# Two-layer attention and expert kernel: expert result rows scattered by token and loaded plainly, instead of gathered by the output stage

## The chip, the cores and the metric

The kernel runs on one core of a Trainium2 chip. A core has five engines with a queue each: TensorE (PE, with its weight loads as PEld), VectorE (DVE), ScalarE (ACT), GpSimd (POOL) and SyncE (SP), and 16 DMA engines that move data on behalf of the queues. The metric is the time of one execution in device microseconds (us): the median of 14 runs is 753.95 us (748.63 to 759.43).

## The reference

Input x has 8 sequences of 512 tokens with 128 channels, all in float32. Two layers follow each other, each `x = x + attention(norm(x)) + experts(norm(x))`.

- Layer 0: a linear attention with a feature map and two states that are multiplied, and a top-1 choice among 8 experts (one 128 x 128 product each, weighted by the router's probability).
- Layer 1: a windowed attention (16 heads, window 32) with a remote part over 64 pooled latents, and a top-2 choice among 8 experts with a hidden layer of 512:

```python
logits = x_flat @ gate_w.T
probs = softmax(logits)
topk_probs, topk_idx = top_k(probs, 2)
hidden = relu(einsum('th,ehf->tef', x_flat, w1) + b1)
all_out = einsum('tef,efh->teh', hidden, w2) + b2
y = sum(gathered(all_out, topk_idx) * topk_probs[:, :, None], axis=1)
```

The change touches the layer-1 experts alone.

## The kernel before, in words

**Stages.** `layer0(b)` (line 626) and `attention1(b)` (line 761) work on one sequence b. The layer-1 experts work on groups of four sequences (GB = 4, line 33), so there are two groups h. `route(h)` (line 968) sorts the 4096 token-and-choice pairs of a group by expert, on the chip: every expert gets a whole number of tiles of 128 rows, 39 tiles in all (TILES, line 35), and the rows of a tile that no token fills are padding. It makes `place_i` (line 1062), which says for every token and choice in which row of the sorted order it lies, and `token_i` (lines 1101 to 1106), which says for every sorted row which token it comes from. `token_i` comes out of a one-hot product `inv` (lines 1073 to 1099): for each sorted row the token's number in its block of 128 ("within") and the number of the block ("tile").

`experts1(h)` (line 1112) goes over the 39 tiles. For each four tiles it gathers the input rows by token from `x_rows` in DRAM (four indirect DMAs on POOL, tile `xgt`, lines 1153 to 1163) and transposes them on PE (`tpx`). For each tile SP loads the weights of its expert (`w1` and `w2` of 256 KB, `b2` of 64 KB, lines 1118 to 1151, with three to four buffers each); PE makes the hidden layer `hp` (line 1192), ACT the relu `ht`, PE the product `yp` (line 1207), and DVE adds the bias to it in `ys` (line 1216). Four tiles of `ys` go in one plain store to `y_rows` in DRAM, in sorted order, on SP (lines 1217 to 1222).

`output(b)` (line 1225) is the last stage of a sequence. It gathers, for each of the two choices a and each of the four blocks t of 128 tokens, the rows of `y_rows` that belong to these tokens: eight indirect DMAs on POOL into `yg` (lines 1232 to 1238), 64 in the whole kernel. DVE then adds each block, times its weight `gw`, to x1 (eight instructions a sequence, line 1243), and SP stores x1 to the output (line 1246). As `y_rows` is one tensor of a group, the first gather of a group waits until all its tiles are stored.

**What sets the order.** Every instruction is recorded first (class `Recorder`, line 113; each call goes through line 348, so that almost all instructions have this line in the profile). `Recorder.order` (line 221) then makes the order in which the instructions of all sequences and stages are put into the engines' queues. It takes, at each step, the instruction that can start first by a table of costs (`_duration`, line 354), and among these the one with the lowest rank; an instruction's rank comes from the time window of its stage in a table written by hand (`PLAN`, line 1256). On the chip each queue is worked off strictly in that order. Nothing is waited for except data and buffers.

**Names in the profile.** `xgt` input rows of a tile, `hp`, `ht`, `yp`, `ys` as above; `sc`, `m`, `pt`, `pw`, `pv` the steps of the windowed attention (scores, softmax, transposed weights, masked weights, product); `le`, `rem_p` those of its remote part; `loc`, `aT`, `fp` its last steps; `amx`, `asd`, `ard`, `lrd` the maxima, sums and divisors of the softmaxes; `xg`, `rp`, `gbc` the experts of layer 0.

Of the kernel before, what the change touches and what calls it, by code (L numbers as in the profile page):

```python
# [9 lines left out]
F32 = mybir.dt.float32  # L10
# [8 lines left out]
P = 128  # L19
# [3 lines left out]
E = 8  # L23
# [6 lines left out]
CHUNK = N // NLAT  # L30


GB = 4
GT = GB * NT
TILES = (2 * GB * N + E * (P - 1)) // P
NEG = -1.0e30
SCALE = 1.0 / float(np.sqrt(np.float32(D)))
SCALE_LAT = 1.0 / float(np.sqrt(np.float32(LC // LH)))
# [3 lines left out]
def _columns(widths):  # L42
    at, out = 0, {}
    for name, w in widths:
# [18 lines left out]
        ("before", P), ("iota", P), ("part4", 1), ("chunk4", NFC), ("within", 1), ("tile", GT),  # L63
    ]
)

# [1 line left out]
def _constants():  # L68

    c = np.zeros((P, _CN), np.float32)  # L70
    p = np.arange(P)

    def put(name, a):
        lo, hi = _CCOL[name]
        c[: a.shape[0], lo:hi] = a.reshape(a.shape[0], hi - lo)

    put("ident", np.eye(P))
    put("heads", p[:, None] // D == p[None, :] // D)
    put("head4", (p[:, None] // D) % 4 == np.arange(4)[None, :])
# [12 lines left out]
    put("late", late)  # L92
    put("group", group)
    put("first", np.broadcast_to(E - np.arange(E), (P, NT, E)))
    put("before", p[:, None] < p[None, :])
    put("iota", np.broadcast_to(p, (P, P)))
    put("part4", p[:, None] // NFC)
    put("chunk4", p[:, None] % NFC == np.arange(NFC)[None, :])
    put("within", p)
    put("tile", np.broadcast_to(np.arange(GT), (P, GT)))  # L100
    return c


# [285 lines left out]
def two_layers_kernel(  # L389
# [55 lines left out]
    def ct(name):  # L445
        lo, hi = _CCOL[name]
        return csb[:, lo:hi]
# [170 lines left out]


    middle, late = {}, {}  # L620
    x_rows = [dram.tile([GB * N, C], F32, tag="xr", name=f"x_rows_{h}", bufs=2) for h in range(B // GB)]
    y_rows = [dram.tile([TILES * P, C], F32, tag="yr", name=f"y_rows_{h}", bufs=2) for h in range(B // GB)]
    logits = [keep.tile([P, GT, E], F32, tag="logits", name=f"logits_{h}") for h in range(B // GB)]
    places = {}

    def layer0(b):
# [114 lines left out]

        xn2 = work.tile([P, NT, C], F32, tag="oT", name="xn2" + nm, bufs=1)
        layernorm(xn2, x1, "d" + nm)
        h, hb = divmod(b, GB)
# [223 lines left out]
    def route(h):  # L968


        nm = f"_{h}"
        n2 = 2 * GT
        sh = [P, 2, GT, E]
        pick = small.tile(sh, F32, tag="picked", name="picked" + nm, bufs=1)
# [20 lines left out]
        mm(tot[:, : GT * E], ones, mf)  # L995
        yield

        half = GT // 2
# [63 lines left out]
        place_i = small.tile([P, n2], I32, tag="place_i", name="place_i" + nm)  # L1062
# [12 lines left out]
        for q in range(n2 // step):  # L1075
            ts = slice(q * step, (q + 1) * step)
            ohr = work.tile([P, step, P], BF16, tag="xg0", name=f"ohr{nm}_{q}", bufs=1)
            nc.vector.tensor_tensor(
                ohr, ct("iota").unsqueeze(1).to_broadcast([P, step, P]),
                rf[:, ts].unsqueeze(2).to_broadcast([P, step, P]), ALU.is_equal,  # L1080
            )
            shj = [P, step, TILES]
            ohj = small.tile(shj, BF16, tag="ohj", name=f"ohj{nm}_{q}", bufs=1)
            nc.vector.tensor_tensor(
                ohj, ct("iota")[:, :TILES].unsqueeze(1).to_broadcast(shj),
                jf[:, ts].unsqueeze(2).to_broadcast(shj), ALU.is_equal,
            )
            tw = small.tile([P, 2, step, TILES], BF16, tag="tw", name=f"tw{nm}_{q}", bufs=1)
            t0 = (q * step) % GT
            nc.vector.tensor_scalar_mul(tw[:, 0], ohj, ct("within"))  # L1090
            nc.gpsimd.tensor_tensor(
                tw[:, 1], ohj, ct("tile")[:, t0 : t0 + step].unsqueeze(2).to_broadcast(shj), ALU.mult
            )
# [13 lines left out]
        places[h] = (place_i, token_i, gw, bias, own_i)  # L1107
        yield

    QUAD, AHEAD = 4, 3  # L1110

    def experts1(h):

        nm = f"_{h}"
        _, token_i, _, bias, own_i = places[h]
        ws, xgs, xts, hts, numbers = {}, {}, {}, {}, {}

        def fetch(j):
# [34 lines left out]
        def gather(q):  # L1153
# [8 lines left out]
                )  # L1162
            xgs[q] = xg

        def turn(q):
# [18 lines left out]
        for j in range(TILES + 1):  # L1184
# [20 lines left out]
            if j:  # L1205
                ht, (_, w2k, b2) = hts.pop(j - 1), ws.pop(j - 1)
                yp = bank(f"yp{nm}_{j - 1}")
                for k in range(NFC):
                    mm(
                        yp[:, :C], ht[:, k], w2k[:, k],  # L1210
                        start=k == 0, stop=k == NFC - 1,
                    )
                q, a = divmod(j - 1, QUAD)
                if a == 0:
                    ys = work.tile([P, QUAD, C], F32, tag="ys", name=f"ys{nm}_{q}", bufs=2)
                nc.vector.tensor_add(ys[:, a], yp[:, :C], b2)
                if a == QUAD - 1 or j == TILES:
                    r0 = q * QUAD * P
                    nc.sync.dma_start(
                        y_rows[h][r0 : r0 + (a + 1) * P].rearrange("(t p) c -> p t c", p=P),  # L1220
                        ys[:, : a + 1],
                    )
                yield

    def output(b):

        nm = f"_{b}"
        x1 = late.pop(b)
        h, hb = divmod(b, GB)
        place_i, _, gw, _, _ = places[h]  # L1230
# [18 lines left out]
    def load_next(b):  # L1249
# [16 lines left out]
        "attention1": (  # L1266
            (105, 168), (147, 199), (206, 258), (273, 318),
            (319, 432), (431, 481), (481, 538), (554, 633),
        ),
        "experts1": ((262, 436), (426, 546)),  # L1270
        "output": (
            (413, 488), (441, 502), (481, 482), (436, 471),
            (489, 595), (570, 580), (547, 625), (578, 664),
        ),
    }

    def put(name, stage, arg, at):
        nc.begin(*PLAN[name][at])
        for _ in stage(arg):
            pass  # L1280
# [3 lines left out]
            put("load", load_next, b, b - 1)  # L1284
        put("layer0", layer0, b, b)
    for name, stage, n in (
        ("route", route, B // GB), ("attention1", attention1, B),
        ("experts1", experts1, B // GB), ("output", output, B),
    ):
        for i in range(n):  # L1290
            put(name, stage, i, i)
# [62 lines left out]
```

## Time and profile before

| what | value |
|---|---|
| median of 14 runs | 753.95 us (748.63 to 759.43) |
| the profiled execution: time / span from first to last instruction | 756.32 us / 754.2 us |
| mean granted PE clock | 0.857 of full |
| busy time in the span: PE, PEld | 587.8 us (78%), 435.9 us (58%) |
| DVE, ACT, POOL | 512.7 us (68%), 339.4 us (45%), 379.2 us (50%) |
| moved by DMA | 86.65 MB, mean 115 GB/s |
| the 78 gathers of input rows on POOL: busy, mean of one | 78.5 us, 1006 ns |
| the 64 gathers of result rows on POOL: busy, mean of one | 62.0 us, 969 ns |
| the 64 updates of x1 by `yg` on DVE: busy, mean of one | 30.9 us, 499 ns |

The profile shows one execution. Busy time counts instructions at work; a queue that waits is idle. A row of the timelines gives start and length in us, engine, line, operation, `out<-in` by the program's names, and in brackets the idle time before it and what ended it ("issue" is time in which the engine waited for nothing that the profile shows). The chain of work that ended last goes back from the last instruction, at each step to what released it. Busy shares are means over stages that have different limits, so the tables by stretch matter more than the sums. The time of an indirect DMA on POOL is the making of its descriptors; the landing of the data comes later.

### The profile page before, as it was taken

To read this page: it belongs to the slowest core of one execution; us is meant where nothing else is said; L and a number is where in the kernel's file an instruction comes from. 1 tells how busy PE (TensorE), PEld (TensorE's weight loads), DVE (VectorE), ACT (ScalarE), POOL (GpSimd) and SP (SyncE) were. 2 spreads that over 40 slices of the span, in tenths; PEclk is the share of its full clock that TensorE was granted. 3 is DMA by queue.
4 is the path that set the end of the run, shared out by engine and by line. 5 is a ranking of instruction groups with operands and counts; after the bars stand their busy time and mean duration, and the time that the engine had idled before them with its cause. 6 is when DMAs were issued, how large, how long until landed. Compare 5 with 4: busy or idle time off the path is not lost.

```text
span 754.2 us, 14113 instructions
## 1 busy us (share of the span) xinstructions
PE 587.8 (78%) x4869; PEld 435.9 (58%) x4869; DVE 512.7 (68%) x1258; ACT 339.4 (45%) x877; POOL 379.2 (50%) x376
## 2 busy tenths in 40 slices
PE   4387798868968769889989989887798789797512
PEld 2233454536736435775756768766687668784412
DVE  2736779899699896984888774993529644616662
ACT  2225246344652332582563767443555447353500
POOL 1021132645551357835755345267668875606784
PEclk9687696998896768898999999999969988997555
DMA  4110212112011221445546465966758775771011
GB/s 139 70 42 29 77 51 89 40 54 75 15 43 57 76 78 55 114 129 133 151 114 185 132 194 158 249 165 191 210 149 218 204 206 146 184 199 50 26 47 51
DMA packets 101543, 86.65 MB, mean 115 GB/s; under 512 B 8056, under 2 KB 80576, under 8 KB 101472
## 3 DMA queue, kind: packets, MB, share of 16 engines
q1 hardware_dynamic: 96640, 75.43, 34.3%
q0 software_dynamic: 4544, 9.32, 5.2%
q10 hardware_dynamic: 288, 1.00, 0.4%
q8 instruction: 39, 0.64, 0.3%
q14 instruction: 32, 0.26, 0.1%
HBM read 76.28 MB, written 9.44 MB: 114 GB/s over the span
## 4 chain that ended last, share of the span: by engine, by line
PE 34%; DVE 28%; POOL 13%; ACT 11%; DMA 7%; issue 6%; POOLq 0%; DVEq 0%; ACTq 0%
PE rp L348 5%; PE yp L348 4%; PE hp L348 4%; POOL yg L348 3%; PE hk L348 2%; DVE nt L348 2%; PE rem_p L348 2%; POOL pw L348 2%; DVE k L348 2%; ACT vb L348 2%; POOL xgt L348 2%; DVE x L348 2%; ACT ks L348 2%; DVE nr L348 2%; DVE ks L348 2%
## 5 line engine op out<-in xcount | busy, mean ns | idle before, releaser
L348 ACT ACTIVATE ht<-hp,bias 128x128 f32<-128x128 f32 x312 | 90.9, 370 | 53.9 <-PE hp L348 53.5
L348 POOL DMA_INDIRECT xgt<-x_rows,token_i x78 | 78.5, 1006 | 33.1 <-issue 15.3
L348 POOL TENSOR_TENSOR xg<-xT,gbc 128x512 f32<-128x512 f32 x32 | 44.0, 1375 | 100.7 <-DMA gbc<-gd 65.4
L348 PE MATMUL hp<-xt,w 128*128 128x128 f32 x624 | 88.0, 286 | 7.5 <-DVE m L348 2.3
L348 PEld LDWEIGHTS hp<-xt,w 128*128 128x128 f32 x624 | 79.3, 198 | 19.2 <-issue 6.3
L348 PE MATMUL yp<-w,ht 128*128 128x128 f32 x624 | 86.6, 287 | 0.6 <-ACT ht L348 0.5
L348 POOL DMA_INDIRECT yg<-y_rows,place_i x64 | 62.0, 969 | 45.2 <-DMA y_rows<-ys 19.4
L348 PEld LDWEIGHTS yp<-w,ht 128*128 128x128 f32 x624 | 79.4, 200 | 3.9 <-issue 1.9
L348 PE MATMUL rp<-xg,we_sb 128*128 128x512 f32 x128 | 73.8, 676 | 3.8 <-DVE x2p L348 1.9
L348 PE MATMUL pv<-pw,vb 128*32 128x64 f32 (+1 forms) x1088 | 40.0, 235 | 42.3 <-POOL pw L348 42.0
L348 PEld LDWEIGHTS pv<-pw,vb 128*32 128x32 f32 x1088 | 36.2, 123 | 50.1 <-POOL pw L348 47.2
L348 POOL TENSOR_TENSOR pw<-pt,csb 128x512 f32<-128x512 f32 x32 | 49.0, 1531 | 13.2 <-DVE pt L348 10.7
L348 DVE SCALAR_TENSOR_TENSOR x<-yg,gw,x 128x128 f32<-128x128 f32 x64 | 30.9, 499 | 29.0 <-DMA yg<-y_rows,place_i 28.4
L348 POOL TENSOR_TENSOR m<-m,ard 128x512 f32<-128x512 f32 x32 | 35.4, 1111 | 27.6 <-DVE ard L348 12.4
L348 POOL TENSOR_TENSOR m<-m,amx 128x512 f32<-128x512 f32 x32 | 35.4, 1106 | 27.0 <-DVE amx L348 24.3
L348 POOL TENSOR_TENSOR le<-le,lrd 128x128 f32<-128x128 f32 (+3 forms) x32 | 23.8, 749 | 34.3 <-DVE lrd L348 18.1
L348 ACT ACTIVATE m<-m,zero_b 128x512 f32<-128x512 f32 x32 | 23.1, 724 | 38.2 <-POOL m L348 38.1
L348 DVE TENSOR_TENSOR ys<-yp,b 128x128 f32<-128x128 f32 x78 | 20.9, 275 | 28.3 <-PE yp L348 22.6
L348 DVE TENSOR_TENSOR xg<-xT,gbc 128x512 f32<-128x512 f32 x32 | 25.8, 805 | 20.8 <-PE rp L348 18.7
L348 ACT ACTIVATE le<-le,zero_b 128x128 f32<-128x128 f32 (+3 forms) x32 | 18.0, 562 | 48.2 <-DVE le L348 45.2
L348 ACT COPY vb<-v 32x128 f32<-32x128 f32 x128 | 37.7, 295 | 2.8 <-PE pv L348 1.0
L348 PE MATMUL hk<-xn,ks 128*128 128x129 f32 x128 | 24.1, 364 | 18.7 <-DVE ks L348 18.7
(218 smaller groups left out, 1314.3 us busy)
## 6 DMA issues: line engine op xcount, KB each, us to landing
w<-in_w_dram SPq DMA_DIRECT2D x156, 256.0 KB
gbc<-gd SPq DMA_DIRECT2D x64, 256.0 KB
b<-in_experts_b_dram SPq DMA_DIRECT2D x78, 64.0 KB
y_rows<-ys SPq DMA_DIRECT2D x18, 256.0 KB
x<-in_x_dram SPq DMA_DIRECT2D x8, 256.0 KB
x_rows<-xn SPq DMA_DIRECT2D x8, 256.0 KB
out_dram<-x SPq DMA_DIRECT2D x8, 256.0 KB
xgt<-x_rows,token_i POOLq DMA_INDIRECT x78
```

Of the source, the lines that this page charges most:

```text
L348: r.ENGINES[name], lambda: call(*args, **kwargs), aps[:1], aps[1:], time, delay, shape
```

## The change

- `route` numbers the token blocks of both choices through: the constant "tile" now holds 1 to 32 (choice 0: 1 to 16, choice 1: 17 to 32), where it held 0 to 15 for both. From the same one-hot product it so gets `row_i`, the row of every sorted row in a tensor with two planes (one for each choice) of 2048 rows behind 128 spare rows; padding gives row 0. `token_i` is made from it: minus 2048 for the second plane, minus 128, not under 0. These are six small DVE instructions in place of two. `place_i` is no longer used outside `route`.
- `experts1` has a `ys` for each tile (six buffers) and sends it by an indirect DMA on POOL to the rows `row_i` of `y_rows`: 39 scatters a group in place of 10 plain stores on SP. `y_rows` is a DRAM tensor that the recorder doesn't follow. After the last tile DVE writes one column of each of the last six `ys` and copies it to `done`: that write can't be made before the scatter that reads the `ys` has landed.
- `output` copies `done` into `yg`, so that the loads that overwrite `yg` come after it, and loads the rows of the sequence in two plain transfers of 256 KB on SP, in place of eight gathers on POOL.
- Groups are written as a table (still four and four), and all windows of `PLAN` but "load" have new numbers, so the order of all queues is a new one.

```diff
-GB = 4
-GT = GB * NT
-TILES = (2 * GB * N + E * (P - 1)) // P
+GROUPS = (4, 4)
...
-    put("tile", np.broadcast_to(np.arange(GT), (P, GT)))
+    n = 2 * max(GROUPS) * NT
+    put("tile", np.broadcast_to(1 + np.arange(n), (P, n)))
...
+        y_rows.append(tc.nc.dram_tensor(f"y_rows_{h}", [P + 2 * n * N, C], F32, kind="Internal").ap())
...
-        own_p = small.tile([P, TILES], F32, tag="own_p", name="own_p" + nm, bufs=1)
-        nc.vector.tensor_copy(own_p, inv[:, :TILES])
-        nc.vector.scalar_tensor_tensor(
-            token_i, inv[:, TILES : 2 * TILES], float(P), own_p, ALU.mult, ALU.add
-        )
-        places[h] = (place_i, token_i, gw, bias, own_i)
+        nc.vector.tensor_copy(at_tile, inv[:, : 2 * TILES].rearrange("p (a j) -> p a j", j=TILES))
+        nc.vector.tensor_single_scalar(other, at_tile[:, 1], float(GT) + 0.5, ALU.is_gt)
+        nc.vector.scalar_tensor_tensor(row, at_tile[:, 1], float(P), at_tile[:, 0], ALU.mult, ALU.add)
+        nc.vector.scalar_tensor_tensor(other, other, -float(GT * P), row, ALU.mult, ALU.add)
+        nc.vector.tensor_scalar(token_i, other, -float(P), 0.0, ALU.add, ALU.max)
+        nc.vector.tensor_copy(row_i, row)
+        places[h] = (row_i, token_i, gw, bias, own_i)
...
+        def scatter(j, ys):
+            ids = row_i[:, j : j + 1]
+            def store():
+                tc.nc.gpsimd.indirect_dma_start(
+                    y_rows[h], bass.IndirectOffsetOnAxis(ap=ids, axis=0), ys, None
+                )
+            nc.add("POOL", store, [], [ys, ids], 1.25, 2.4)
+            last[:] = (last + [ys])[-YS:]
...
-                if a == 0:
-                    ys = work.tile([P, QUAD, C], F32, tag="ys", name=f"ys{nm}_{q}", bufs=2)
-                nc.vector.tensor_add(ys[:, a], yp[:, :C], b2)
-                if a == QUAD - 1 or j == TILES:
-                    r0 = q * QUAD * P
-                    nc.sync.dma_start(
-                        y_rows[h][r0 : r0 + (a + 1) * P].rearrange("(t p) c -> p t c", p=P),
-                        ys[:, : a + 1],
-                    )
+                ys = work.tile([P, C], F32, tag="ys", name=f"ys{nm}_{j - 1}", bufs=YS)
+                nc.vector.tensor_add(ys, yp[:, :C], b2)
+                scatter(j - 1, ys)
                 yield
+        for i, ys in enumerate(last):
+            nc.vector.memset(ys[:, :1], 0.0)
+            nc.vector.tensor_copy(done[:, i : i + 1], ys[:, :1])
+        written[h] = done
+        yield
...
         yg = work.tile([P, 2, NT, C], F32, tag="yg", name="yg" + nm, bufs=1)
+        nc.vector.tensor_copy(yg[:, 0, 0, :YS], written[h])
+        rows = y_rows[h][P:].rearrange("(a t p) c -> p a t c", a=2, p=P)
         for a in range(2):
-            for t in range(NT):
-                col = a * GT + hb * NT + t
-                nc.gpsimd.indirect_dma_start(
-                    yg[:, a, t], None, y_rows[h],
-                    bass.IndirectOffsetOnAxis(ap=place_i[:, col : col + 1], axis=0),
-                )
+            nc.sync.dma_start(yg[:, a], rows[:, a, hb * NT : (hb + 1) * NT])
...
         "layer0": (
-            (41, 43), (57, 70), (60, 174), (113, 194),
-            (180, 254), (261, 270), (310, 335), (331, 344),
+            (51, 52), (82, 83), (80, 130), (83, 164),
+            (147, 220), (253, 290), (276, 338), (361, 362),
         ),
-        "route": ((230, 231), (348, 407)),
+        "route": ((211, 216), (399, 444)),
...
-        "experts1": ((262, 436), (426, 546)),
+        "experts1": ((238, 447), (481, 579)),
         "output": (
-            (413, 488), (441, 502), (481, 482), (436, 471),
-            (489, 595), (570, 580), (547, 625), (578, 664),
+            (465, 533), (442, 443), (474, 493), (524, 525),
+            (639, 692), (562, 577), (584, 585), (661, 740),
         ),
```

In the order that this makes, the last expert product of the second group stands ahead of most of attention of sequence 7, as before, and now also ahead of the last steps of attention of sequence 6; sequence 7's first projections (q, k and the latent ones) stand ahead of it now.

More of the change, by code (lines that the diff above doesn't have):

```diff
@@ L30, with _tiles @@
 CHUNK = N // NLAT
-GB = 4
-GT = GB * NT
-TILES = (2 * GB * N + E * (P - 1)) // P
+GROUPS = (4, 4)
+GROUP_OF = [(h, i) for h, n in enumerate(GROUPS) for i in range(n)]
+def _tiles(n):
+    return (2 * n * N + E * (P - 1)) // P
 NEG = -1.0e30
@@ L62 @@
         ("first", NT * E),
-        ("before", P), ("iota", P), ("part4", 1), ("chunk4", NFC), ("within", 1), ("tile", GT),
+        ("before", P), ("iota", P), ("part4", 1), ("chunk4", NFC), ("within", 1), ("tile", 2 * max(GROUPS) * NT),
     ]
@@ L620, in two_layers_kernel @@
     middle, late = {}, {}
-    x_rows = [dram.tile([GB * N, C], F32, tag="xr", name=f"x_rows_{h}", bufs=2) for h in range(B // GB)]
-    y_rows = [dram.tile([TILES * P, C], F32, tag="yr", name=f"y_rows_{h}", bufs=2) for h in range(B // GB)]
-    logits = [keep.tile([P, GT, E], F32, tag="logits", name=f"logits_{h}") for h in range(B // GB)]
+    x_rows, y_rows, logits = [], [], []
+    for h, n in enumerate(GROUPS):
+        x_rows.append(dram.tile([n * N, C], F32, tag=f"xr{h}", name=f"x_rows_{h}", bufs=1))
+        y_rows.append(tc.nc.dram_tensor(f"y_rows_{h}", [P + 2 * n * N, C], F32, kind="Internal").ap())
+        logits.append(keep.tile([P, n * NT, E], F32, tag=f"logits{h}", name=f"logits_{h}", bufs=1))
     places = {}
@@ L743, in layer0 @@
         layernorm(xn2, x1, "d" + nm)
-        h, hb = divmod(b, GB)
+        h, hb = GROUP_OF[b]
         nc.sync.dma_start(
@@ L971, in route @@
         nm = f"_{h}"
+        GT, TILES = GROUPS[h] * NT, _tiles(GROUPS[h])
         n2 = 2 * GT
@@ L996, in route @@
         yield
-        half = GT // 2
+        half = 1
+        while 2 * half < GT:
+            half *= 2
         run = small.tile([P, 2, half + GT, E], F32, tag="run", name="run" + nm, bufs=1)
@@ L1061, in route @@
         nc.vector.tensor_reduce(place, both.rearrange("p a t e -> p (a t) e"), AX.X, ALU.add)
-        place_i = small.tile([P, n2], I32, tag="place_i", name="place_i" + nm)
+        place_i = small.tile([P, n2], I32, tag="place_i", name="place_i" + nm, bufs=1)
         nc.vector.tensor_copy(place_i, place)
@@ L1088, in route @@
             tw = small.tile([P, 2, step, TILES], BF16, tag="tw", name=f"tw{nm}_{q}", bufs=1)
-            t0 = (q * step) % GT
             nc.vector.tensor_scalar_mul(tw[:, 0], ohj, ct("within"))
             nc.gpsimd.tensor_tensor(
-                tw[:, 1], ohj, ct("tile")[:, t0 : t0 + step].unsqueeze(2).to_broadcast(shj), ALU.mult
+                tw[:, 1], ohj, ct("tile")[:, ts].unsqueeze(2).to_broadcast(shj), ALU.mult
             )
@@ L1100, in route @@
             yield
-        token_i = small.tile([P, TILES], I32, tag="token_i", name="token_i" + nm)
-        own_p = small.tile([P, TILES], F32, tag="own_p", name="own_p" + nm, bufs=1)
-        nc.vector.tensor_copy(own_p, inv[:, :TILES])
-        nc.vector.scalar_tensor_tensor(
-            token_i, inv[:, TILES : 2 * TILES], float(P), own_p, ALU.mult, ALU.add
-        )
-        places[h] = (place_i, token_i, gw, bias, own_i)
+        at_tile = small.tile([P, 2, TILES], F32, tag="at_tile", name="at_tile" + nm, bufs=1)
+        nc.vector.tensor_copy(at_tile, inv[:, : 2 * TILES].rearrange("p (a j) -> p a j", j=TILES))
+        other = small.tile([P, TILES], F32, tag="own", name="other" + nm, bufs=1)
+        nc.vector.tensor_single_scalar(other, at_tile[:, 1], float(GT) + 0.5, ALU.is_gt)
+        row = small.tile([P, TILES], F32, tag="row", name="row" + nm, bufs=1)
+        nc.vector.scalar_tensor_tensor(row, at_tile[:, 1], float(P), at_tile[:, 0], ALU.mult, ALU.add)
+        nc.vector.scalar_tensor_tensor(other, other, -float(GT * P), row, ALU.mult, ALU.add)
+        token_i = small.tile([P, TILES], I32, tag="token_i", name="token_i" + nm)
+        nc.vector.tensor_scalar(token_i, other, -float(P), 0.0, ALU.add, ALU.max)
+        row_i = small.tile([P, TILES], I32, tag="row_i", name="row_i" + nm)
+        nc.vector.tensor_copy(row_i, row)
+        places[h] = (row_i, token_i, gw, bias, own_i)
         yield
-    QUAD, AHEAD = 4, 3
+    QUAD, AHEAD, YS = 4, 3, 6
+    written = {}
     def experts1(h):
         nm = f"_{h}"
-        _, token_i, _, bias, own_i = places[h]
+        TILES = _tiles(GROUPS[h])
+        row_i, token_i, _, bias, own_i = places[h]
         ws, xgs, xts, hts, numbers = {}, {}, {}, {}, {}
@@ L1163, in gather @@
             xgs[q] = xg
+        last = []
+        def scatter(j, ys):
[6 more added lines that the diff above has]
+            last[:] = (last + [ys])[-YS:]
         def turn(q):
@@ L1212, in experts1 @@
                     )
-                q, a = divmod(j - 1, QUAD)
-                if a == 0:
-                    ys = work.tile([P, QUAD, C], F32, tag="ys", name=f"ys{nm}_{q}", bufs=2)
-                nc.vector.tensor_add(ys[:, a], yp[:, :C], b2)
-                if a == QUAD - 1 or j == TILES:
-                    r0 = q * QUAD * P
-                    nc.sync.dma_start(
-                        y_rows[h][r0 : r0 + (a + 1) * P].rearrange("(t p) c -> p t c", p=P),
-                        ys[:, : a + 1],
-                    )
-                yield
+                ys = work.tile([P, C], F32, tag="ys", name=f"ys{nm}_{j - 1}", bufs=YS)
+                nc.vector.tensor_add(ys, yp[:, :C], b2)
+                scatter(j - 1, ys)
+                yield
+        done = small.tile([P, YS], F32, tag="done", name="done" + nm)
+        for i, ys in enumerate(last):
[3 more added lines that the diff above has]
+        yield
     def output(b):
@@ L1228, in output @@
         x1 = late.pop(b)
-        h, hb = divmod(b, GB)
-        place_i, _, gw, _, _ = places[h]
+        h, hb = GROUP_OF[b]
+        gw = places[h][2]
         yg = work.tile([P, 2, NT, C], F32, tag="yg", name="yg" + nm, bufs=1)
+        nc.vector.tensor_copy(yg[:, 0, 0, :YS], written[h])
+        rows = y_rows[h][P:].rearrange("(a t p) c -> p a t c", a=2, p=P)
         for a in range(2):
-            for t in range(NT):
-                col = a * GT + hb * NT + t
-                nc.gpsimd.indirect_dma_start(
-                    yg[:, a, t], None, y_rows[h],
-                    bass.IndirectOffsetOnAxis(ap=place_i[:, col : col + 1], axis=0),
-                )
+            nc.sync.dma_start(yg[:, a], rows[:, a, hb * NT : (hb + 1) * NT])
         yield
@@ L1261, in two_layers_kernel @@
         "layer0": (
[L1262 to L1263 removed]
+            (51, 52), (82, 83), (80, 130), (83, 164),
+            (147, 220), (253, 290), (276, 338), (361, 362),
         ),
[L1265 removed]
+        "route": ((211, 216), (399, 444)),
         "attention1": (
[L1267 to L1268 removed]
+            (73, 158), (135, 163), (191, 290), (292, 348),
+            (358, 454), (459, 547), (527, 615), (606, 628),
         ),
[L1270 removed]
+        "experts1": ((238, 447), (481, 579)),
         "output": (
[L1272 to L1273 removed]
+            (465, 533), (442, 443), (474, 493), (524, 525),
+            (639, 692), (562, 577), (584, 585), (661, 740),
         ),
@@ L1286, in two_layers_kernel @@
     for name, stage, n in (
-        ("route", route, B // GB), ("attention1", attention1, B),
-        ("experts1", experts1, B // GB), ("output", output, B),
+        ("route", route, len(GROUPS)), ("attention1", attention1, B),
+        ("experts1", experts1, len(GROUPS)), ("output", output, B),
     ):
```

## The prediction

> **What bounds the kernel now.** I read the page first (busy shares, slices, chain), then the time of each engine by stretch, then the POOL, DVE and PE timelines of the end.
>
> ```profile
> PE 34%; DVE 28%; POOL 13%; ACT 11%; DMA 7%; issue 6%; POOLq 0%; DVEq 0%; ACTq 0%
> ...
> L348 POOL DMA_INDIRECT xgt<-x_rows,token_i x78 | 78.5, 1006 | 33.1 <-issue 15.3
> ...
> L348 POOL DMA_INDIRECT yg<-y_rows,place_i x64 | 62.0, 969 | 45.2 <-DMA y_rows<-ys 19.4
> ```
>
> No engine is full: the chain of work that ended last lies 34% on PE, 28% on DVE, 13% on POOL. The second line is the gather of the experts' input rows (78, unchanged), the third the gather of their result rows (64, removed). The table by stretch tells where each engine has room; its columns are stretch, length, busy time of PE, PEld, DVE, ACT and POOL (with counts), granted clock, DMA share, GB/s:
>
> ```profile
> 300.00:520.00 220.00, 192.47 (x1701) 151.22 (x1701) 169.69 (x422) 121.20 (x329) 118.94 (x111) 0.97 0.57 159
> 520.00:677.50 157.50, 135.70 (x1364) 120.33 (x1363) 78.50 (x175) 83.68 (x251) 98.49 (x102) 0.92 0.69 191
> 677.50:754.20 76.70, 34.19 (x343) 24.76 (x341) 40.14 (x86) 17.80 (x43) 49.66 (x51) 0.59 0.16 44
> ```
>
> From 300 to 677.5 us PE is busy 328 of 377.5 us: this is the expert stage, and PE sets its pace. At 677.1 us the last expert product (yp of tile 38) ends, and a tail of 754.2 - 677.1 = **77.1 us** follows, with PE busy 34 of it at clock 0.59. In the tail stand attention of sequence 7 and the outputs of sequences 4 to 7. What holds it is POOL's in-order queue:
>
> ```profile
> 689.20 0.94 POOL L348 DMA_INDIRECT yg<-y_rows,place_i  x1 [0.31 <-issue]
> 690.17 0.98 POOL L348 TENSOR_TENSOR le<-le,lrd 128x128 f32<-128x128 f32 x2
> ...
> 718.98 1.04 POOL L348 TENSOR_TENSOR m<-m,amx 128x512 f32<-128x512 f32 x1
> 720.18 1.26 POOL L348 DMA_INDIRECT yg<-y_rows,place_i  x1 [0.16 <-issue]
> ...
> 727.98 0.94 POOL L348 DMA_INDIRECT yg<-y_rows,place_i  x1 [0.30 <-issue]
> 728.94 1.27 POOL L348 TENSOR_TENSOR pw<-pt,csb 128x512 f32<-128x512 f32 x1
> ...
> 743.05 0.95 POOL L348 DMA_INDIRECT yg<-y_rows,place_i  x1 [0.30 <-issue]
> 744.02 1.27 POOL L348 TENSOR_TENSOR aT<-aT,loc 128x512 f32<-128x512 f32 x1
> ```
>
> Between the lines for 720.18 and 727.98 stand five more gathers at 1.25 us from start to start. And DVE at the same time:
>
> ```profile
> 718.05 0.71 DVE L348 STREAM_TRANSPOSE pt<-m 128x512 f32<-128x512 f32 x1 [1.36 <-POOL m L348]
> ...
> 729.34 2.03 DVE L348 SCALAR_TENSOR_TENSOR x<-yg,gw,x 128x128 f32<-128x128 f32 x1 [0.95 <-DMA yg<-y_rows,place_i]
> ...
> 738.63 0.69 DVE L348 SCALAR_TENSOR_TENSOR loc<-gsb,pv 128x512 f32<-128x512 f32 x1 [3.16 <-PE pv L348]
> ```
>
> The transposed weights pt were there at 718.76, POOL was done with m at 720.02, but pw begins at 728.94: seven gathers, **8.9 us**. loc was there at 739.32, aT begins at 744.02: **4.7 us**. By the same reading pw at 735.34 lost 0.6 us (pt there at 734.68) and m at 716.97 lost 1.5 us (ard there at 715.50). Sum 15.7 us. The late le at 690.17 (its divisor was there at 685.38) I don't count: see below.
>
> **The change, part by part.** The sum is made against the profiled execution: 756.3 us, of which the span is 754.2; that is 0.3% above the median of 753.95, so a difference goes over to the median as it is.
>
> *The tail.* All 32 gathers leave it; the order built for the changed kernel leaves POOL there with 22 instructions and the last scatter or two. Two plain loads per sequence, on SP, take the gathers' place. They wait for the last six scatters, through a chain that wasn't there: ys of tile 38 is ready 0.3 us after the last product; its scatter stands behind one pw (1.3 us) and takes 1.0 us; landing 2.3 us (the gather at 684.20 released its reader 3.26 us after its start; bounds 2.06 us for the plain y_rows store at 677.47 and 5.31 us for the xgt gather at 514.34); the two small DVE copies 0.3; load issue 0.4 and landing 3 (out at the end 3.4, a w load 5.98 at most). That is 8.6 to 9.6 us after the last product for sequence 5. In DVE's queue the eight updates of sequence 5 (8 x 0.35 = 2.8) and loc of sequence 6 (0.7) stand behind that wait, and all softmax steps of sequence 7 behind those: they begin 13.2 us after the last product, where they begin 14.2 us after it now (copy_predicated at 691.27). So the new wait takes the place of the late le: gain 1.0. From there DVE has the same work as now (33 us busy of 59.7), and 15.7 us of POOL delay go. Of attention of sequence 6 its last two pv (about 1 us each), aT and fp now lie after the last product, but in the first 14 us, where PE has room; its add (0.7) is extra. Tail: -1.0 - 15.7 + 0.7 = **-16**. Bounds: -5 (landings at the long ends, +3 and +3, and DVE updates of 2.03 us beside POOL as at 729.34, some 3 of them) and -27 (DVE's 31 us and few waits).
>
> *POOL in the expert stage.* 39 scatters of 1.25 us a group come in; a scatter is the same instruction as a gather, so I take 0.97 us plus 0.3 issue (bounds 0.94, and 2.01 for the longest xgt). From 520 to 677.5, 32 gathers leave and 39 come: +9 us on POOL, no change on PE. From 300 to 520 nothing leaves: +49 us on an engine that is 119 of 220 busy. About 60 POOL steps there have a reader waiting (le, m, pw, aT of 2.5 sequences, xg and the norms of three): 60 x 49/220 x 0.6 us (half a scatter) = 8 us, half of it on PE's path: **+4**; bounds 0 and +25 (each scatter that waits for its ys stops what is behind it; now PE waits 25 us for POOL in all from 310 to 677).
>
> *Weights.* The order of the second group changes: after its first tile come tiles 1 to 16 with little attention between (two pv, one sc, two projections), where now attention 5 and 6 lie between. On PE that is 17 x 1.79 (start of hp to start of hp, 663.56 to 667.13, two tiles) + 10 = 41 us. The queues must move 28 weight blocks of 256 KB, 13 of 64 KB, gathers and scatters of 64 KB a tile, and the first group's loads and stores, 3 MB: 13 MB. The best stretch of the trace moved 260 GB/s, the last dense one 205:
>
> ```profile
> 470.00:480.00 10.00, 8.95 (x101) 8.52 (x101) 9.37 (x28) 5.33 (x20) 4.41 (x5) 1.00 1.00 260
> 550.00:560.00 10.00, 10.00 (x95) 9.66 (x94) 2.70 (x6) 5.18 (x19) 4.71 (x6) 0.50 0.39 118
> 650.00:677.50 27.50, 24.06 (x269) 22.94 (x264) 8.01 (x20) 14.04 (x47) 6.74 (x5) 1.00 0.77 205
> ```
>
> At 260 GB/s 50 us, **+9**; at 205 GB/s 63 us, +22; below, 0 if what PE waits for elsewhere hides it. I take +9, by the stretch whose DMA share is 1.00.
>
> *A stall that goes.* At 550 to 560 PE ran at clock 0.50 (line above), after it had waited for le of sequence 5, which POOL ran at 546.13 behind gathers: 10 us for 5 us of work. Those gathers go: **-5**, bounds 0 and -8.
>
> *Small parts.* Three more dependent DVE steps of 0.2 us per routing: +1. Two small DVE steps for each of the last six tiles and one per output: some 32 x 0.13 = 4 us in a DVE that is 79 of 157 busy: 0 as long as the scatters have landed when DVE comes to them; if not, ys, lmx and copy_predicated queue behind them, and PE for these. ys has six buffers instead of two of four: a tile takes 157/39 = 4 us, so a landing under 24 us stops nothing. SP: 20 stores leave, 16 loads come; behind the first load's wait stand out of sequence 1 and the weights of tile 3, whose buffer is only free after tile 0's product anyway: 0, else up to 5.
>
> Sum: -16 + 4 + 9 - 5 + 1 = **-7**: 749.3 for the profiled execution, 747 against the median.
>
> **A rule against the row.** Gathers beside a busy DVE took 0.94 to 1.26 us in the output stage, mean 0.97: hardly lengthened. The Trainium skill, page "SBUF — State Buffer", section on the "DVE blocks DMA" trap, says that GpSimd cannot write a DMA's descriptors while a DVE copy in a two-port mode holds the shared port. By it each scatter could last one DVE copy longer (0.7 us for the longest here), 78 x 0.7 = 55 us more on POOL, and the change would lose. The rows decide against that; the rule would show as scatters well over 1.3 us.
>
> **Rivals.** (1) *The middle is free*: weights and POOL hide in waits that are there anyway: -16 - 5 + 1 = -20, 734. For it: PE idles 49 us from 300 to 677.5. Against: DMA share of 0.77 and 1.00 in dense stretches. (2) *The tail's gain is given back*: scatters land late or DVE becomes the bound with its updates in front of the softmax steps: half of the 16 goes, -7 + 8 = +1, 755. It decides from a landing of some 8 us. (3) *Slower*: the weight queue becomes the bound in tiles 0 to 17 of the second group; at 205 GB/s +22 instead of +9: -7 + 13 = +6, **760**; at 170 GB/s (76 us, +35) 773. It decides once that stretch takes over 57 us on the clock, 16 over PE's work. Against it: 260 GB/s were reached. (4) *It doesn't do what it says*: all padding lanes write one row of y_rows; if those writes follow one another, the last scatters of a group land late: that is (2).
>
> **How the numbers follow.** About 0.5% (3.8 us) is what a measurement of this kernel tells from no change, so 750.2 and 757.7 are the borders. Forecast 747 (741 to 750): 0.30. Rival 1, 734 (under 741): 0.28. Rivals 2 and 4, 755 (750 to 758): 0.15. Rival 3, 760 and over: 0.27. Hence faster 0.58, same 0.15, slower 0.27. The range leaves 0.1 on each side: 729, where the tail's bound adds to rival 1, to 770, nearly rival 3's far end.
>
> **What would show it.** Right: after the last yp the span has some 61 us left, POOL's pw and aT there follow pt and loc at once, the first copy_predicated stands about 13 us after the last yp. Wrong: scatters over 1.3 us; PE waits for w over 10 us between tiles 1 and 17; PE's wait for pw above 25 us before the last product; DVE waiting for scatters at the small copies; the last yp later than 690 us.

## The result and the profile after

The changed kernel takes 824.95 us (median of 10 runs, 818.82 to 829.52) where the kernel before takes 752.63 (47 runs): ratio **1.095** [1.091, 1.098]. It is 9.5% slower, and 78 us over the forecast of 747. In two of the four series in which the experiments ran, the kernel before took 789 and 792 us instead of 754 to 756, so each run is held against others of its own series wherever tens of us matter.

The span of the profiled execution is 822.5 us. Two rows of its groups (operation, count, busy time, mean of one, then idle time just before them and what ended most of it):

```profile
L1191 POOL DMA_INDIRECT y_rows<-ys,row_i x78 | 80.8, 1036 | 159.9 <-DMA y_rows<-ys,row_i 72.8
L354 POOL DMA_INDIRECT xgt<-x_rows,token_i x78 | 77.5, 994 | 30.8 <-issue 17.1
```

A scatter costs POOL what a gather costs (1036 and 994 ns), as forecast. New is the 160 us that POOL stands idle in front of scatters, and what ended the largest named part of it, 73 us: the landing of *another scatter of the same tensor*. POOL's table of waits (total, times, longest) and the summary of y_rows (from the start of a scatter to its landing) say the same:

```profile
POOL y_rows L1191 <- DMA y_rows<-ys,row_i: 72.8, 20, 6.3
```

```profile
DMA to landing us min/median/max: 2.2/3.5/7.1
```

The 73 us are not all of it. The trace holds the landing of the scatter before for 61 of the 76 scatters that have one before them in their group. None of the 61 begins before that landing, and 37 begin 0.73 to 0.81 us after it; POOL's idle time in front of these 37 adds up to 112 us, though the profile puts part of it down to other instructions that ended at about the same time.

The longest turn of it, on POOL:

```profile
611.53 1.00 POOL L1191 DMA_INDIRECT y_rows<-ys,row_i  x1 [0.30 <-issue]
612.83 0.96 POOL L354 DMA_INDIRECT xgt<-x_rows,token_i  x1 [0.30 <-issue]
619.37 0.99 POOL L1191 DMA_INDIRECT y_rows<-ys,row_i  x1 [5.58 <-DMA y_rows<-ys,row_i]
620.39 1.06 POOL L354 TENSOR_TENSOR m<-m,ard 128x512 f32<-128x512 f32 x1
```

And on DVE at the same time:

```profile
609.15 0.29 DVE L354 TENSOR_TENSOR ys<-yp,b 128x128 f32<-128x128 f32 x1 [0.21 <-PE yp L354]
...
621.48 0.71 DVE L354 STREAM_TRANSPOSE pt<-m 128x512 f32<-128x512 f32 x1 [8.19 <-POOL m L354]
622.12 0.25 DVE L354 TENSOR_TENSOR ys<-yp,b 128x128 f32<-128x128 f32 x1
...
622.88 0.48 DVE L354 TENSOR_TENSOR ys<-yp,b 128x128 f32<-128x128 f32 x2
```

The ys of 609.15 (the ninth of its group, as the scatter of 619.37 is) was ready at 609.44, but its scatter starts at 619.37: it waits until the scatter of 611.53 has landed, after 7.1 us, the longest landing of all. POOL works its queue in order, so the softmax step m of an attention behind it starts at 620.39 only; DVE waits 8.19 us for m, and three ys additions stand behind that transposition in DVE's queue. On PE the late steps of the softmax show most. Its wait for pw ahead of the last expert product, in the kernel before and in the changed one (over the whole span the two are alike, 42.0 and 39.2 us, as the tail has less of it now):

```profile
PE pv L348 <- POOL pw L348: 15.1, 12, 2.8
...
PE pv L354 <- POOL pw L354: 26.9, 11, 7.5
```

The table by stretch (stretch, length, busy time of PE, PEld, DVE, ACT and POOL with counts, granted clock, DMA share, GB/s) tells where the time went:

```profile
300.00:520.00 220.00, 182.04 (x1487) 139.55 (x1486) 145.48 (x373) 107.61 (x288) 123.17 (x118) 0.93 0.48 140
...
560.00:760.00 200.00, 136.55 (x1176) 118.34 (x1176) 68.71 (x168) 78.33 (x240) 98.52 (x103) 0.84 0.51 142
760.00:822.50 62.50, 36.11 (x413) 28.87 (x413) 41.55 (x96) 16.44 (x41) 26.34 (x24) 0.58 0.18 53
```

The last yp ends at 758.1 us where it ended at 677.1: **+81**. The tail behind it is 64.4 us where it was 77.1: **-12.7**. From 300 us to the last yp PE is busy 343.7 of 458.1 us, where it was busy 327.8 of 377.1: of the 81 us, 65 are idle time and 16 are longer busy time. The granted clock of the expert stretch is lower: 0.93 and 0.84, where 300 to 520 had 0.97 and 520 to 677.5 had 0.92. PE busy in the whole span grows from 587.8 to 611.1 us for the same 4869 records.

### The profile page after: what moved, and what is told of

The parts are those of the page before. It is cut to its first block, busy times and chain, and to the rows that moved or that the text cites. A ratio compares the mean times of both kernels' runs of the same rounds, so it can differ in the third digit from the quotient of the medians.

```text
span 822.5 us, 14186 instructions
## 1 busy us (share of the span) xinstructions
PE 611.1 (74%) x4869; PEld 454.5 (55%) x4869; DVE 505.0 (61%) x1298; ACT 338.4 (41%) x877; POOL 390.5 (47%) x390
## 5 line engine op out<-in xcount | busy, mean ns | idle before, releaser
L1191 POOL DMA_INDIRECT y_rows<-ys,row_i x78 | 80.8, 1036 | 159.9 <-DMA y_rows<-ys,row_i 72.8
L354 PE MATMUL hp<-xt,w 128*128 128x128 f32 x624 | 94.4, 302 | 23.8 <-DVE m L354 15.1
L354 PEld LDWEIGHTS hp<-xt,w 128*128 128x128 f32 x624 | 86.3, 213 | 37.2 <-DVE m L354 15.3
L354 PE MATMUL yp<-w,ht 128*128 128x128 f32 x624 | 90.1, 295 | 12.6 <-ACT ht L354 12.5
L354 PEld LDWEIGHTS yp<-w,ht 128*128 128x128 f32 x624 | 82.4, 207 | 18.9 <-ACT ht L354 14.1
L354 PE MATMUL pv<-pw,vb 128*32 128x64 f32 (+1 forms) x1088 | 43.7, 249 | 39.6 <-POOL pw L354 39.2
L354 PEld LDWEIGHTS pv<-pw,vb 128*32 128x32 f32 x1088 | 39.9, 134 | 50.4 <-POOL pw L354 44.2
L354 PE MATMUL sc<-kT,qe 32*128 32x64 f32 x1024 | 41.3, 304 | 5.0 <-DVE le L354 2.2
L354 DVE STREAM_TRANSPOSE pt<-m 128x512 f32<-128x512 f32 x32 | 22.6, 705 | 36.5 <-POOL m L354 33.1
L354 PEld LDWEIGHTS sc<-kT,qe 32*128 32x128 f32 x1024 | 38.1, 215 | 10.7 <-issue 3.7
```

Source lines behind the costliest of these rows:

```text
L354: r.ENGINES[name], lambda: call(*args, **kwargs), aps[:1], aps[1:], time, delay, shape
L1191: tc.nc.gpsimd.indirect_dma_start(y_rows[h], bass.IndirectOffsetOnAxis(ap=ids, axis=0), ys, None)
```

## The experiments

My theory from this trace (theory 1): as the rows of a scatter are only known on the chip, the framework takes every scatter for a write of the whole of y_rows and puts it after the previous one's landing. In the changed kernel's trace, 70 of the 76 scatters with one before them have a recorded wait for the semaphore by which that one tells its landing. The planner doesn't know of these waits, since `scatter` records no write (`nc.add("POOL", store, [], [ys, ids], 1.25, 2.4)`). The rivals: theory 2, the new order; theory 3, a scatter is dearer than a gather for POOL or the DMA queues; theory 4, padding lanes that all write row 0 land late.

**e1, e8, e12: no chain** (one kernel, run in three series). `dram_disjoint_views` gives handles of one DRAM tensor that the framework takes for disjoint; the loads of `output` still come after the copy of `done`, as in the changed kernel. Padding lanes get spare rows of their own behind the planes, so that the views' promise is true.

```diff
+    views = [dram_disjoint_views(y_rows[h], _tiles(GROUPS[h])) for h in range(len(GROUPS))]
...
-                    y_rows[h], bass.IndirectOffsetOnAxis(ap=ids, axis=0), ys, None
+                    views[h][j], bass.IndirectOffsetOnAxis(ap=ids, axis=0), ys, None
...
-        nc.vector.tensor_copy(row_i, row)
+        nc.vector.tensor_scalar(spare, ct("iota")[:, :TILES], float(P), float(P + GT * 2 * P), ALU.mult, ALU.add)
+        nc.vector.tensor_scalar(spare, spare, ct("within"), None, ALU.add)
+        nc.vector.tensor_single_scalar(other, at_tile[:, 1], 0.5, ALU.is_lt)
+        nc.vector.tensor_mul(spare, spare, other)
+        nc.vector.tensor_add(row_i, row, spare)
```

> The changed kernel, with every scatter written through its own view of y_rows, so that no scatter waits for the one before it; and with padding rows sent to spare rows of their own (row 0 took them all), since without that two scatters in flight could write the same row. Windows and costs as in the changed kernel. Theory 1 (each scatter waits on POOL until the previous scatter has landed, and le, m, pw and the gathers stand behind it): the 73 us of POOL's waits for scatters go and most of the 75 us come back, time 735 to 765, last yp before 700 us. Theory 2 (the new order is what costs: weights come late where tiles stand close together): 810 or over, PE still waits for w. Theory 3 (a scatter itself costs POOL or the DMA queues more than a gather): 800 or over, with POOL busy and landings as now.

Measured: 745.1 us (e1), beside 820.2 for e2 and 792.1 for the kernel before. Then e8, beside the changed kernel (e6):

> e1 once more, beside the others on one chip: 738 to 750, and its ratio to the kernel before depends on what that takes there: 0.985 to 0.995 where the kernel before takes 753.

> The changed kernel, unchanged, beside the others on one chip: 815 to 830, whatever the kernel before takes there.

Measured: e8 750.2, e6 831.6 (just over its range), the kernel before 789.2. And e12 with e14, beside 754.2 for the kernel before:

> e1 once more, on another chip if one comes: it took 745 and 750 where the kernel before took 792 and 789; where the kernel before takes 753 to 757, the question is whether e1 is ahead (738 to 748, the prediction's case with the chain gone) or level (750 to 760).

> The changed kernel unchanged, beside e12 and e13 on one chip: 818 to 833.

Measured: **e12 738.5** (ratio to the kernel before 0.979 [0.973, 0.986]), **e14 829.8** (1.099 [1.092, 1.106]). Theory 1 holds three times over: without the waits 75, 81 and 91 us are gone. What is left is some 2% faster than the kernel before in e12's series; held against 752.6, e1 and e8 would be 1.0% and 0.3% faster. In e12's trace the scatter is as long as ever, landings are no shorter (13 of 78 are recorded), no scatter has a recorded wait for the one before, and PE hardly waits for weights:

```profile
L1198 POOL DMA_INDIRECT y_rows<-ys,row_i x78 | 80.4, 1031 | 48.1 <-DVE ys L355 26.4
```

```profile
DMA to landing us min/median/max: 2.3/4.5/6.8
```

```profile
PE hp L355 <- DMA w<-in_w_dram: 1.2, 1, 1.2
```

```profile
543.00:673.00 130.00, 113.89 (x1129) 101.58 (x1127) 55.98 (x143) 74.68 (x231) 91.38 (x93) 0.95 0.72 207
```

From its first yp to its last the second group (39 tiles) takes 131 us (542.8 to 674.1), where the changed kernel takes 190 (568.6 to 758.1), and the clock is 0.95 instead of 0.84. Theory 3 falls: scatters cost POOL the same, and landings are as long. Theory 2 falls too: e1 has the new windows and is fast. The steps of `spare` shift its order somewhat against the changed kernel's, but not against e2's (next).

**e2: spare rows alone**, chain kept: the diff of `row_i` above, without views.

> The changed kernel with padding rows sent to spare rows of their own, and the wait of each scatter for the one before it kept. Theory 1: 818 to 830, no change, landing of scatters about 3.4 us as now. Theory 4 (all padding lanes write one row, those writes follow one another, and so scatters land late): landings fall by 1 us or more, POOL's wait for scatters from 73 us to under 45, time under 800.

Measured: 820.2 us (a single run), POOL idle before scatters 143 us (160 in the changed kernel). Its trace holds no landings, and the split of the idle time by releaser (36 us put down to a scatter's landing) is therefore thinner; the time decides, and it is within 1% of the changed kernel's 825. Theory 4 falls.

e2 and e1 are also the cleanest pair for theory 1. The instructions of PE and POOL stand in the same order in both traces (4869 and 390 of them), so that only the waits differ: 65 of 76 scatters have a recorded wait for the one before in e2, none in e1. Scatters, and the second group from its first yp to its last, in e2 and then in e1:

```profile
L1196 POOL DMA_INDIRECT y_rows<-ys,row_i x78 | 80.2, 1028 | 143.1 <-DMA y_rows<-ys,row_i 36.3
...
L1198 POOL DMA_INDIRECT y_rows<-ys,row_i x78 | 80.2, 1028 | 52.3 <-DVE ys L355 29.2
```

```profile
578.30:754.70 176.40, 121.21 (x1139) 107.62 (x1138) 56.47 (x139) 74.95 (x231) 90.83 (x92) 0.85 0.54 153
...
542.40:680.50 138.10, 121.87 (x1139) 107.47 (x1139) 58.38 (x145) 74.27 (x231) 92.53 (x94) 0.93 0.68 196
```

PE is busy for as long in both stretches (121.2 and 121.9 us), so that the 38 us between their lengths are idle time. Ahead of the last yp PE waits 43.7 us for pw in e2 and 6.1 in e1. So in this order the chain costs 75 us; the 81 and 91 us of the other two comparisons have the other order and the spread between runs in them too.

**e3: two views by turns** (`views[h][j % 2]`), so that each scatter waits for the last but one.

> As e1, but with two views by turns: each scatter waits for the one before the last. Theory 1: two landings of 3.4 us can lie beside each other and the mean distance of scatters is 4 to 5 us, so nearly all waits go: POOL waits 5 to 25 us for scatters, time 740 to 780, between e1 and the changed kernel and nearer to e1. Theories 2 and 3: 800 or over.

Measured: 749.9 us beside e1's 745.1; idle before scatters 61 us, beside 52 in e1, and 3.3 us of it put down to a landing. One scatter more in flight is nearly the whole cure, as landings of 3.5 us and a scatter every 3.5 us (median in e3's second group) let one expect.

**e4, e5: the order alone.** e4 is the kernel before with the table of windows of the changed kernel; e5 is the kernel before.

> The kernel before (plain stores, gathers at the end) with the table of windows of the changed kernel. Theory 1: the order alone costs little, 745 to 785. Theory 2: 800 or over, with PE waiting for w in the second group as in the changed kernel.

> The kernel before, unchanged, to have its profile on a chip of the experiments: there it took 792 us in the first call, where its record is 753. If that chip's engines or clock are slower for every program, all groups are longer by some 5% and the changed kernel would be too (it was not: 820 with spare rows, against 825). If one of its own waits is longer there, one group of waits holds some 38 us more than the 754.2 us profile shows, and it should be one that the changed kernel doesn't have: the gathers of y_rows or the stores they wait for.

Measured: e4 788.2 us beside 792.1 for the kernel before; e5 786.3, with a span of 784.2. Both are single runs. Held against its own series, the new order costs the old data path nothing that one run could show. e5 doesn't settle why the kernel before took 790: the order of its instructions is that of the 754.2 us profile, its last yp is 26 us later, and from 560 to 660 its granted clock is 0.67 to 0.83 in four of five stretches of 20 us, where the other profile has 0.82 to 1.00. It isn't the chip: the series of e8 and that of e12 ran on the same one. What sets it off stays open.

**e7: the data path alone**: e1 with the windows of the kernel before.

> e1 (a view for each scatter, padding to spare rows) with the table of windows of the kernel before: the data path alone, on nearly the old order. If the new windows matter little, 735 to 755 as e1 has 745. If they were what spares the weights' queue or the tail, 760 or over. If the old ones fit the new path better, under 735.

Measured: 770.2 us beside e8's 750.2. The new windows are worth 20 us to the new path (by what, no run shows), and nothing to the old one as far as e4's one run tells.

**e9, e13: a planner that knows of the chain.** One line, in the changed kernel (e9) and in e1 (e13):

```diff
-            nc.add("POOL", store, [], [ys, ids], 1.25, 2.4)
+            nc.add("POOL", store, [y_rows[h]], [ys, ids], 1.3, 3.4)
```

> The changed kernel with its chain of scatters kept, but the planner is told of it: each scatter is recorded as a write of y_rows with a delay of 3.4 us (2.4 before) and 1.3 us of POOL, so that the order puts scatters apart and other POOL work between them. If the loss comes from an order that didn't know of the wait, POOL's waits for scatters fall from 73 us to under 40 and the time to 760 to 795. If the chain itself is the limit (a scatter's issue, landing and wake take some 4.7 us, and 39 of them in a group 183 us, against 135 us that e1's second group takes), 795 to 825.

> e9's order (planner told that scatters follow one another) with e1's views, so that no scatter waits on the chip: what is left of the chain once the order allows for it. POOL waited 27 us for scatters in e9 and DVE 17 us for ys: 740 to 755, 5 to 15 under e9. If e9's order is itself longer, within 5 us of e9.

Measured: e9 **759.2 us**, just under its range (ratio 1.005 [1.001, 1.008]; the kernel before took 756.1), e13 745.5 (0.989 [0.986, 0.993]). My floor of 183 us for a group was wrong for the products: e9's second group takes 160 us from its first yp to its last (546 to 705). Its scatters do take 173 us (547 to 720), but the last of them run on beside the tail. With the chain still in place, the waits for landings shrink from 72.8 to:

```profile
POOL y_rows L1191 <- DMA y_rows<-ys,row_i: 26.7, 19, 3.3
```

and here is how, on POOL:

```profile
622.57 1.01 POOL L1191 DMA_INDIRECT y_rows<-ys,row_i  x1 [0.15 <-issue]
623.88 0.98 POOL L354 DMA_INDIRECT xgt<-x_rows,token_i  x1 [0.30 <-issue]
...
627.69 1.00 POOL L1191 DMA_INDIRECT y_rows<-ys,row_i  x1 [0.30 <-issue]
...
633.13 1.00 POOL L1191 DMA_INDIRECT y_rows<-ys,row_i  x1 [0.16 <-issue]
634.15 1.07 POOL L354 TENSOR_TENSOR m<-m,ard 128x512 f32<-128x512 f32 x1
```

Scatters stand 5 us apart with gathers and softmax steps between, and none of these three waits for a landing. So the chain costs 75 us in an order that was made without it (e2 to e1) and some 12 to 14 in one made with it (e9 to e13, by their ratios and by their times; they ran in two series, and the orders of the two differ somewhat).

**e10: gathers back in the output stage**: e1 with eight indirect DMAs a sequence in place of the two loads; the spare rows stay behind the planes, which now begin at row 0.

```diff
-            nc.sync.dma_start(yg[:, a], rows[:, a, hb * NT : (hb + 1) * NT])
+            for t in range(NT):
+                col = a * GROUPS[h] * NT + hb * NT + t
+                nc.gpsimd.indirect_dma_start(
+                    yg[:, a, t], None, y_rows[h][: 2 * GROUPS[h] * N],
+                    bass.IndirectOffsetOnAxis(ap=places[h][5][:, col : col + 1], axis=0),
+                )
```

> e1 with one part undone: the output stage gets its rows by eight indirect DMAs on POOL again (from the planes, in order; the spare rows lie behind the planes), in place of two plain loads. The step of the prediction that takes 15.7 us of POOL gathers out of the tail: 755 to 770, with a tail after the last yp of 70 us or more. If POOL had room there anyway: under 752, tail 63 to 66 us.

Measured: 796.7 us, far over the range, and 47 to 58 more than e1 took in its three series. The last yp ends at 702.1, 28 us after e12's, and the tail is 89.3 us where e12 has 63.4. DVE, then POOL in that tail:

```profile
722.03 0.71 DVE L355 STREAM_TRANSPOSE pt<-m 128x512 f32<-128x512 f32 x1 [0.31 <-POOL m L355]
...
722.14 0.98 POOL L355 DMA_INDIRECT yg<-y_rows,plain_i  x1
...
730.92 0.94 POOL L355 DMA_INDIRECT yg<-y_rows,plain_i  x1 [0.31 <-PE vj L355]
731.88 1.27 POOL L355 TENSOR_TENSOR pw<-pt,csb 128x512 f32<-128x512 f32 x1
```

Eight gathers take 9.7 us, and pw, whose pt was there at 722.74, stands behind them until 731.88. So the step of the tail is there, and undoing it costs the tail 26 us. The 28 us ahead of the last yp were not expected; the order of e10's queues is another than e1's, and no run shows what of them is the gathers' own.

**e11: views in the second group alone.**

> e2 (spare rows, chain kept) with the views in the second group alone. The chain's cost by group: the first group took 240 us from its first to its last product in e2 and 216 in e1, the second 205 and 136. If the costs add up, 765 to 780. If one late group makes the other late, under 755 or over 790.

Measured: 768.6 us in the series of e9 and e10, with the order of e1 and e2. The first group's last yp ends at 542 us (545 in e2, 515 in e1); from there to the last yp of the second group it takes 163 us, as e1 does (165), where e2 takes 210 (from its first yp to its last e2's second group takes 176 us, not the 205 that I had written). The costs of the two groups add up.

## Why the prediction was wrong

**The tail: right, a little too large.** Forecast: some 61 us left after the last yp, first copy_predicated 13 us after it. The changed kernel:

```profile
756.98 1.16 PE L354 MATMUL yp<-w,ht 128*128 128x128 f32 x8
```

```profile
762.68 0.99 POOL L1191 DMA_INDIRECT y_rows<-ys,row_i  x1 [1.09 <-DVE done L354]
...
766.17 0.06 DVE L354 MEMSET ys<- 128x1 f32 x1
...
766.47 0.90 DVE L354 COPY yg<-done 128x6 f32<-128x6 f32 x1
...
774.65 0.77 DVE L354 COPY_PREDICATED m<-csb,sc 128x256 f32<-128x256 int32 x2
```

The yp ends at 758.14. The write that waits for the last scatter comes 8.0 us later, the copy that lets the loads go follows at once, and copy_predicated begins 16.5 us after the yp instead of 13.2. The tail is 64.4 us: -12.7 where I had -16. Of the missing 3.3 us, 2.9 are in the start of the last scatter: I had it 1.6 us after the last product, and it starts 4.5 us after it. On DVE the last ys ends 2.5 us after the product (760.66) instead of 0.3, behind a transposition and a mask step, and POOL then waits until 0.75 us after the landing of the scatter before (761.93): the chain reaches into the tail too. e10 shows the cause that I named, POOL's gathers ahead of pw.

**POOL in the expert stage: the step that failed.** I wrote +4, bounds 0 and +25, because "a scatter is the same instruction as a gather". As an instruction it is: 998 ns at the median, 994 ns the mean gather. But gathers read, and the gathers of one tensor here do not wait for one another (in the kernel before they stand 1.25 us apart); scatters write, and the framework puts two writes whose rows it doesn't know one after the other. The second sentence that failed is in the small parts: "ys has six buffers ... a landing under 24 us stops nothing". The buffer isn't what the next scatter waits for. A median landing of 3.5 us stops it, because the next scatter is due some 3.5 us later and, in an order that doesn't know of the wait, is often put sooner. The chain alone is +74 in the last yp with the order held (754.7 in e2, 680.5 in e1), and +84 from e12 to the changed kernel (674.1, 758.1): three times my upper bound. I asked of each scatter what it costs and what its ys waits for, and not what else it waits for. Two of my signs of being wrong came with it: the last yp was later than 690 us, and PE waited over 25 us for pw ahead of it (26.9).

**Weights +9: not there.** PE waits 1.2 us for w in e12 and 7.6 in the changed kernel, and the second group's stretch moves 207 GB/s in e12, near the lower of my two rates. The 41 us that I had for PE in tiles 1 to 17 were for tiles closer together than they came to stand: in e12 they take 54 us (first hp of tile 1 at 541.9, of tile 17 at 596.0). Rival 3 fell with it: slower it was, by another cause.

**The stall at 550 to 560 (-5) and the routing (+1)** can't be read apart from the weights, nor from the scatters' own time on POOL, which e12 has too. Together the four are -3 in e12 (last yp 677.1 before, 674.1 in e12) where I had +9.

**The sum.** Without the chain it is -3 and -13.7 (tail 63.4), -17 us, in e12's profile, and -11 and -12 in those of e1 and e8 (spans 743.1 and 742.6), where I had -7 and rival 1 had -20. So what I saw of the change was mostly right and somewhat too dark; what I left out was larger than all of it. Rival 4 (padding) fell in e2. Rival 2 had the mechanism nearest to this one, late scatters, but with its place in the tail and a point of 8 us: here landings of 3.5 us were enough, about the distance between scatters, and the place is the middle.

**The rule I set against the row** (the Trainium skill, page "SBUF — State Buffer", the "DVE blocks DMA" trap) would have shown as scatters well over 1.3 us. In the changed kernel they were 952 ns at the fastest and 1036 in the mean, with three of 78 over 1.3 us and the longest at 2570: the row was the better guide here.

## What to carry to other kernels

Before indirect writes replace indirect reads, ask what each write waits for besides its data: here a destination that is only known on the chip made every write wait for the landing of the one before, and on an in-order queue this held up all that stood behind. Views that are declared disjoint (with rows that really are) took the wait away; two in flight already did nearly all of it. If the wait has to stay, tell it to the planner: the chain cost 75 us in an order made without it and some 12 to 14 in one made with it.

## What the runs showed that I had not expected

- Landings of scatters of 64 KB took 2.2 us at least, 3.5 at the median and 7.1 at most in the changed kernel, beside weight loads. The Trainium skill, page "DMA: Bandwidth & Descriptors", section "Anatomy of one DMA — SWDGE (gpsimd) path", gives about 2.0 us plus the bytes at 436 GB/s, which for 64 KB would be an estimate of 2.15 us: here that is near the shortest landing, not the usual one. A chain reckoned with it would have come out over a third too short.
- The plain loads of 256 KB of y_rows landed after 6.3 us at the median in the changed kernel, where w loads of the same size took 3.7.
- With the chain on POOL the granted TensorE clock was lower too: from 300 us to the last yp 0.86 in e2 and 0.94 in e1, which has the same order. PE's busy time in the whole span differed with it: 611.6 us and 597.5.
